# Expert blocks taken two at a time, by seven half-size products in each layer

## The chip, the core and the metric

The kernel runs on one core of one Trainium2 chip. The metric is the device time of one execution, in microseconds; 3 runs of the kernel before gave a median of 2139.81 us, from 2139.24 to 2141.18. All matrices are float32.

## What is computed

A gated cross-attention layer is followed by a gated mixture of experts. Batch is 32, with 112 query rows and 375 context rows each, 256 features wide; there are 16 heads of 64.

```python
x = x + tanh(g_xattn) * attention(context, layernorm(x))   # 16 heads, 487 keys per batch
xf = layernorm(x).reshape(3584, 256)
scores, idx = top_k(softmax(xf @ gate_w), 2)               # 2 of 8 experts per token
h = gelu(xf @ w1[e] + b1[e])                               # 256 -> 1024
y = h @ w2[e] + b2[e]                                      # 1024 -> 256
x = x + tanh(g_ffn) * (scores / sum(scores)) . y[idx]
```

The router sends 7168 rows (3584 tokens, two experts each) to the experts. Evaluated on these inputs, the reference's counts for experts 0 to 7 are 953, 854, 759, 878, 866, 1158, 921 and 779.

## The kernel before

The kernel has two stages, and TensorE's work is written out by hand in one order for the whole kernel. Each other engine, and the SyncE queue (SP) that issues nearly all DMAs, also executes in the order of the program text.

The attention stage is a loop over n = 0 to 127 (32 batches times 4 head groups). Each n has scores, softmax, transposes of the attention, and one part of the key and value projections, in five slots h = 0 to 4 (`slots`, `pe` and `dve` hold what each slot issues). The projections already work on two batches at once by seven products (`seven`, L346): seven products of half-size blocks and a number of sums give what eight products would. Their sums are made on GpSimd (`add`, L394: `kT` and `vv`) and VectorE (L404, L408, L418). Every 128 finished tokens form a slab; `project`, `residual` and `normed` make its attention output, `logits_of` (L577) its eight router logits, and `route_parts` finds its two experts, its gates and its rows' places. An indirect DMA on GpSimd's queue (L673) scatters the rows to `xg` in DRAM, one region for each expert.

The expert stage works on blocks of 128 rows of one expert. 60 blocks always run, and 3 more stand behind a condition at the end (on these inputs the eight counts, rounded up to blocks, come to 60). For a block t, `fetch_rows` (L875) loads its rows from `xg`; `turn_rows` (L893) turns them by two TensorE transposes; `hidden` (L906) makes 8 chunks of 128 hidden features, each a sum of two matmuls with 128 moving columns, and ScalarE applies Gelu while it empties PSUM (L913); `second` (L919) makes 8 matmuls with 256 moving columns into one PSUM tile; VectorE adds the bias (L929) and multiplies by the gate (L935); an indirect DMA on GpSimd's queue adds the rows to the output (L936). In float32 the profile records each matmul twice, and each transpose once. `run` orders TensorE's work as `hidden(t)`, `turn_rows(t + 1)`, `second(t - 1)`.

Expert weights lie in three buffer sets (`weights_of`), used in turn by t % 3. `fetch_weights` (L888) loads w1, b1, w2 and b2 of a block's expert, 1024 KB each for w1 and w2, two blocks ahead. Blocks stand in order of expert, and a DMA is skipped by a condition when its set already holds the expert.

The first six blocks' experts and rows are fixed while attention still runs (`locate_early`). The rest wait for the last two slabs (26 and 27): after the last attention step TensorE runs `project`, the hidden and second layers of blocks 0 to 3 and the router of these slabs, then `locate_late`; the rows of blocks 6 to 9 are fetched, and the regular loop begins.

```python
for t in range(begin, end):
    hidden(t)
    if t + 1 < end:
        turn_rows(t + 1)
    if t > begin or follow:
        second(t - 1)
        combine(t - 1)
```

Of the kernel before, what the change touches and what calls it, by code (L numbers as in the profile page):

```python
# [9 lines left out]
I32 = mybir.dt.int32  # L10
# [13 lines left out]
def kernel(  # L24
# [36 lines left out]
    NSLOT = 2 * T // P + E - 1  # L61
    NE = 6
    NB = 3
    SURE = NSLOT - 3
    AHEAD = 4
# [33 lines left out]
    gwd = dram.tile([E, D], F32, name="gwd")  # L99

# [9 lines left out]
    for e in range(E):  # L110
# [31 lines left out]
    )  # L142

    sums = {
        tag: [const.tile([P, E + 4], F32, name=f"sums{tag}_{n}") for n in range(4)] for tag in "ab"
    }
    for tag in "ab":
        for n in range(4):
            nc.gpsimd.memset(sums[tag][n], 0.0)
# [16 lines left out]
    if True:  # L166
# [20 lines left out]
        lnrows = wqp.tile([4 * KD, P], F32, name="lnrows")  # L187
        b1rows = wqp.tile([E * NF, P], F32, name="b1rows")
        slot = wqp.tile([P, P], F32, name="slot")
# [404 lines left out]
        def route_parts(g, eng):  # L594
# [101 lines left out]
            def stranger_hits(j, e):  # L696
                v["hit"] = rt.tile([P, 2, P], F32, tag="hit", name=f"hit_{j}_{e}", bufs=1)
                nc.vector.tensor_tensor(
                    v["hit"],
                    slot.unsqueeze(1).to_broadcast([P, 2, P]),  # L700
                    v["far"][:, j, e : e + 2].unsqueeze(2).to_broadcast([P, 2, P]),
                    ALU.is_equal,
                )
# [51 lines left out]
        def whole_blocks(tag, rows_, less, up):  # L755
# [6 lines left out]
            nc.vector.tensor_single_scalar(whole, whole, -P, op=ALU.bitwise_and)  # L762
            size = sums[tag][0]
            nc.vector.tensor_copy(size[:, 4:], whole)
# [5 lines left out]
            return size[:, 4:], sums[tag][3][:, 3:]  # L770

        def located(tag, first, start, last):
# [6 lines left out]
            nc.vector.tensor_scalar(begun, first[:, :E], row, None, ALU.is_le)  # L779
# [5 lines left out]
            nc.vector.tensor_tensor(step, start, first[:, :E], ALU.subtract)  # L785
            nc.vector.tensor_tensor(step, step, begun, ALU.mult)
            nc.vector.tensor_reduce(one, step, AX.X, ALU.add)
            nc.vector.tensor_tensor(where[:, 1:2], one, row, ALU.add)
            yield
            nc.vector.tensor_scalar(one, row, float(-NB * P), None, ALU.add)  # L790
            nc.vector.tensor_scalar(begun, first[:, :E], one, None, ALU.is_le)
            nc.vector.tensor_reduce(one, begun, AX.X, ALU.add)
            if last is not None:
                nc.vector.tensor_tensor(one, one, last, ALU.add)
# [3 lines left out]
            if last is not None:  # L798

                nc.vector.tensor_tensor(one, row, first[:, E : E + 1], ALU.is_lt)  # L800
# [6 lines left out]
            found["ab".index(tag)] = wherei  # L807
# [3 lines left out]
        def locate_early():  # L811


            full, first = whole_blocks("a", found.pop("ps"), None, 0.0)
            taken = mp.tile([P, E], F32, name="taken")
            nc.vector.tensor_scalar(
                taken, first[:, :E], -1.0, float(NE * P), ALU.mult, ALU.add
# [3 lines left out]
            found["taken"] = taken  # L821
# [3 lines left out]
            yield from located("a", first, eoff, None)  # L825
            yield

            last = found["last"] = mp.tile([P, 1], F32, name="last")
            begun = mp.tile([P, E], F32, name="begunl")
            nc.vector.tensor_scalar(last, row, float((NE - NB) * P), None, ALU.add)  # L830
            nc.vector.tensor_scalar(begun, first[:, :E], last, None, ALU.is_le)
            nc.vector.tensor_reduce(last, begun, AX.X, ALU.add)
            nc.vector.tensor_scalar(begun[:, :1], row, float(NB * P), None, ALU.is_lt)
            nc.vector.tensor_tensor(last, last, begun[:, :1], ALU.mult)
            yield

        def locate_late():
            _, first = whole_blocks("b", found.pop("ps"), found["taken"], float(P - 1))
            for _ in located("b", first, found["start"], found["last"]):
                pass  # L840


        weights_of = []

        def weight_buffers(pool, n):
            weights_of.append(
                (
                    pool.tile([P, KD, FF], F32, name=f"w1_{n}"),
                    pool.tile([P, NF], F32, name=f"b1_{n}"),
                    pool.tile([P, NF, D], F32, name=f"w2_{n}"),  # L850
                    pool.tile([P, D], F32, name=f"b2_{n}"),
                )
            )

        xs, xsT, hid, psy, ys = {}, {}, {}, {}, {}

        def number(t, n, most, engines=(ET.SP,)):
            late, i = (0, t) if t < NE else (1, t - NE)
            return nc.values_load(  # L859
                found[late][i : i + 1, n : n + 1],  # L860
# [5 lines left out]

        def fetch_rows(t):
            r = number(t, 1, PADS)

            i, new = (t - NE) % (AHEAD + 1 + NE), AHEAD + 1  # L870
            if t < NE or i >= new:
                xs[t] = found["early"].tile([P, C], F32, tag="xs", name=f"xs_{t}", bufs=NE)
            else:
                xs[t] = found["rows"].tile([P, C], F32, tag="xs", name=f"xs_{t}", bufs=new)
            nc.sync.dma_start(xs[t], xg[bass.ds(r, P), :])  # L875

        def fetch_weights(t):

            e = number(t, 0, E - 1)
            new = {"cond": number(t, 2, 1)} if t >= NB else {}  # L880
            w1t, b1t, w2t, b2t = weights_of[t % NB]
            for dst, src in (
                (w1t, w1[bass.ds(e, 1)].rearrange("o (k p) f -> p (o k) f", p=P)),
                (b1t, b1d[bass.ds(e, 1)].rearrange("o p c -> p (o c)")),
                (w2t, w2[bass.ds(e, 1)].rearrange("o (c p) d -> p (o c) d", p=P)),
                (b2t, b2[bass.ds(e, 1), :].to_broadcast([P, D])),
            ):
                nc.sync.dma_start(dst, src, **new)  # L888

        def turn_rows(t, copy=None):  # L890
            ps = ps_m.tile([P, KD, P], F32, tag="m", name=f"ps_x_{t}")
            for k in range(KD):
                nc.tensor.transpose(ps[:, k, :], xs[t][:, k * P : (k + 1) * P], ident)  # L893
            xsT[t] = found["tiles" if t > 0 else "early"].tile(
                [P, KD, P], F32, tag="xsT", name=f"xsT_{t}"
            )
            (copy or nc.vector.tensor_copy)(xsT[t], ps)

        def hidden(t, lo=0, hi=NF):
            w1t, b1t, _, _ = weights_of[t % NB]  # L900
            if lo == 0:
                hid[t] = found["tiles"].tile([P, NF, P], F32, tag="h", name=f"h_{t}")
            for f in range(lo, hi):
                ps = ps_m.tile([P, P], F32, tag="m", name=f"ps_h_{t}_{f}")
                for k in range(KD):
                    nc.tensor.matmul(  # L906
                        ps,
                        lhsT=w1t[:, k, f * P : (f + 1) * P],
                        rhs=xsT[t][:, k, :],
# [3 lines left out]
                nc.scalar.activation(hid[t][:, f, :], ps, AF.Gelu, bias=b1t[:, f : f + 1])  # L913

        def second(t):
            w2t = weights_of[t % NB][2]
# [14 lines left out]
        def combine(t):  # L931
            if t not in ys:
                biased(t)
# [399 lines left out]
```

## Time and profile before

| what | value |
|---|---|
| median of 3 runs | 2139.81 us |
| the profiled execution | 2140.79 us |
| its span | 2139.1 us |
| mean granted TensorE clock | 0.997 |
| busy PE, weight loads (PEld) | 2111.2 us, 1660.0 us |
| busy VectorE (DVE), ScalarE (ACT), GpSimd (POOL) | 1249.4, 1206.4, 708.5 us |
| moved by DMA | 142.63 MB, mean 67 GB/s |

Busy time is the time in which an engine executes. A row of a group gives the line, the engine, the operation, output and inputs, how often it ran, its busy time, the mean length of one in ns, and the idle time ahead of it with what ended that idle time. Starts that follow each other more closely than the mean length show that instructions overlap, so that the pace of a stream is read from the timeline.

### The profile page before, as it was taken

The page shows a single profiled execution, that of the slowest core. Times are in us where ns is not written, and L with a number is a line of the kernel's source. Part 1 is how long each engine was busy: PE and PEld are TensorE (multiplying, and loading weights), DVE is VectorE, ACT ScalarE, POOL GpSimd, SP SyncE. Part 2 cuts the span into 40 slices and gives each one's busy share as a digit, 9 for nine tenths or more (in the row PEclk, how much of TensorE's full clock was granted, in tenths as well). Part 3 has the DMA queues.
Part 4 walks back from the last instruction along what each step waited for, and adds up shares of the span by engine and source line. Part 5 has one row for each costly group of instructions (what it writes and reads, how often), then busy time and mean ns, then how long its engine had stood idle before and what let it go on. Part 6 is the DMA issues. An engine that isn't in the chain of part 4 may idle for free. (4 is left out here: it accounts for less than half of the span.)

```text
span 2139.1 us, 41500 instructions
## 1 busy us (share of the span) xinstructions
PE 2111.2 (99%) x15944; PEld 1660.0 (78%) x15944; DVE 1249.4 (58%) x2784; ACT 1206.4 (56%) x2887; POOL 708.5 (33%) x992
## 2 busy tenths in 40 slices
PE   9999999999999999999999999999999999999998
PEld 5777777777777777777777777777777889999997
DVE  6667676767676767676767676766768521111111
ACT  5666566656665666656656666665655433434433
POOL 4532323343333423442425332533323222222222
PEclk9999999999999999999999999999999999999999
DMA  6693000010000000000000000000002377655552
GB/s 149 183 321 105 18 13 18 13 28 20 16 13 25 25 18 13 30 18 16 13 18 23 28 13 27 14 23 6 6 6 83 102 210 211 166 161 162 155 138 59
DMA packets 116896, 142.63 MB, mean 67 GB/s; under 512 B 15088, under 2 KB 104120, under 8 KB 116568
## 3 DMA queue, kind: packets, MB, share of 16 engines
q1 hardware_dynamic: 104232, 123.57, 18.6%
q0 software_dynamic: 11328, 15.33, 3.9%
q8 instruction: 127, 2.08, 0.4%
q10 hardware_dynamic: 1136, 1.05, 0.2%
q14 instruction: 73, 0.60, 0.1%
HBM read 166.84 MB, written 48.99 MB: 101 GB/s over the span
## 5 line engine op out<-in xcount | busy, mean ns | idle before, releaser
L483 ACT ACTIVATE ex<-ex,rc 112x487 f32<-112x487 f32 x512 | 331.1, 694 | 328.2 <-DVE rc L481 323.3
L459 DVE TENSOR_REDUCE nmx<-ps_s 112x2 f32<-112x974 f32 x256 | 288.0, 1167 | 312.7 <-PE ps_s L449 311.7
L469 ACT ACTIVATE ex<-ps_s,nmx 112x487 f32<-112x487 f32 x512 | 337.2, 666 | 159.7 <-DVE nmx L459 159.0
L490 PEld LDWEIGHTS ps_t<-ident,ex 112*122 112x122 f32 x2048 | 231.8, 138 | 118.3 <-issue 96.9
L913 ACT ACTIVATE h<-ps_h,b 128x128 f32<-128x128 f32 x480 | 175.5, 367 | 260.5 <-PE ps_h L906 220.0
L490 PE MATMUL ps_t<-ident,ex 112*122 112x112 f32 x2048 | 280.8, 259 | 0.2 <-DVE exT L494 0.2
L494 DVE COPY exT<-ps_t 122x448 f32<-122x448 f32 x384 | 237.4, 618 | 37.8 <-PE ps_t L490 36.6
L449 PE MATMUL ps_s<-kT,qT 64*112 64x487 f32 x1024 | 242.0, 591 | 0.0
L394 POOL TENSOR_TENSOR vv<-tmpv,vv 122x512 f32<-122x512 f32 x64 | 81.2, 1269 | 471.9 <-ACT vv L412 377.2
L504 PEld LDWEIGHTS ps_o<-exT,vv 122*64 122x64 f32 (+1 forms) x4096 | 197.6, 136 | 44.7 <-DVE kT L408 32.2
L906 PEld LDWEIGHTS ps_h<-xsT,w 128*128 128x128 f32 x1920 | 224.2, 192 | 6.7 <-ACT h L913 1.8
L906 PE MATMUL ps_h<-xsT,w 128*128 128x128 f32 x1920 | 226.3, 275 | 2.7 <-ACT h L913 1.2
L919 PE MATMUL ps_y<-w,h 128*128 128x256 f32 x960 | 218.6, 381 | 0.0
L504 PE MATMUL ps_o<-exT,vv 122*64 122x112 f32 (+1 forms) x4096 | 211.4, 260 | 0.0
L384 PE MATMUL ps_v<-wkv_s,tT 128*122 128x128 f32 x1536 | 202.0, 274 | 1.2 <-DVE vv L408 1.2
L936 POOL DMA_INDIRECT out_dram<-y,xs x60 | 93.6, 1559 | 314.7 <-DVE y L935 179.4
L919 PEld LDWEIGHTS ps_y<-w,h 128*128 128x128 f32 x960 | 179.3, 192 | 22.4
L378 PE MATMUL ps_k<-tT,wkv_s 128*128 128x487 f32 x378 | 189.4, 583 | 3.4 <-ACT qT L317 3.3
L384 PEld LDWEIGHTS ps_v<-wkv_s,tT 128*122 128x122 f32 x1536 | 181.9, 185 | 4.0 <-issue 1.8
L384 PEld LDWEIGHTS ps_v<-wkv,kvT 128*122 128x122 f32 x1024 | 125.9, 185 | 74.3 <-issue 56.7
L394 POOL TENSOR_TENSOR kT<-tmpk,kT 128x487 f32<-128x487 f32 x63 | 76.9, 1220 | 316.5 <-ACT kT L412 316.4
L418 DVE TENSOR_TENSOR kT<-ps_k,kT 128x487 f32<-128x487 f32 x189 | 124.7, 660 | 47.7 <-PE ps_k L378 42.6
(215 smaller groups left out, 3125.3 us busy)
## 6 DMA issues: line engine op xcount, KB each, us to landing
w<-in_L_ffn_w_dram SPq DMA_DIRECT2D x120, 1024.0 KB
xg<-pad SPq DMA_DIRECT2D x8, 3640.0 KB
cin<-in_ctx_dram SPq DMA_DIRECT2D x32, 336.0 KB
xs<-xg SPq DMA_DIRECT2D x60, 130.0 KB
b<-in_L_ffn_b_dram SPq DMA_DIRECT2D x60, 128.0 KB
xin<-in_x_dram SPq DMA_DIRECT2D x32, 112.0 KB
x<-in_x_dram SPq DMA_DIRECT2D x28, 128.0 KB
out_dram<-x SPq DMA_DIRECT2D x28, 128.0 KB
```

Of the source, the lines that this page charges most:

```text
L378: nc.tensor.matmul(ps, lhsT=w[:, 0, i * P : (i + 1) * P], rhs=x[:, :NK], start=True, stop=True)
L384: nc.tensor.matmul(ps[:, c, :], lhsT=x[:, c * KC : (c + 1) * KC], rhs=w[:, 1, i * P : (i + 1) * P], start=True, stop=True,)
L449: nc.tensor.matmul(ps[:, j, :NK], lhsT=qT[b // 2, i][r, b % 2, :], rhs=kT[b, i][r, :], start=True, stop=True,)
L459: nc.vector.tensor_reduce(nmx[b, i], pss[b, i][:, :, :NK], AX.X, ALU.max, negate=True)
L469: nc.scalar.activation(t[:, j, :NK], ps[:, j, :NK], AF.Exp, bias=nmx[b, i][:, j : j + 1], accum_out=sm[b, i][:, j : j + 1],)
L483: nc.scalar.mul(ex[b, i][:, j, :NK], ex[b, i][:, j, :NK], rc[:, j : j + 1])
L490: nc.tensor.transpose(ps[:, c, :], ex[b, i][:, j, c * KC : (c + 1) * KC], ident[:S, :S])
L494: (nc.scalar.copy if h == 2 else nc.vector.tensor_copy)(exT[b, i, j], ps)
L504: nc.tensor.matmul(ps[y * DH : (y + 1) * DH, r, x * S : (x + 1) * S], lhsT=vv[j][:m, c, x, r, y * DH : (y + 1) * DH], rhs=exT[2 * g + x, i ...
L906: nc.tensor.matmul(ps, lhsT=w1t[:, k, f * P : (f + 1) * P], rhs=xsT[t][:, k, :], start=(k == 0), stop=(k == KD - 1),)
L913: nc.scalar.activation(hid[t][:, f, :], ps, AF.Gelu, bias=b1t[:, f : f + 1])
L919: nc.tensor.matmul(psy[t], lhsT=hid[t][:, f, :], rhs=w2t[:, f, :], start=(f == 0), stop=(f == NF - 1),)
```

## The change

Rows of one expert are taken in 21 pairs of 128-row blocks and 18 single blocks (plus 3 behind the condition). The first 13 pairs (table "a") are placed from the router's counts of 20 slabs, the next 8 (table "b") and the singles (table "c") from the full counts. Each table lists its units in order of expert. Pair 0 is done by plain matmuls with 256 moving columns (`hidden_plain`, `second_plain`). Pairs 1 to 20 use seven products in each layer: `hidden_pair` makes seven products of four matmuls each, 128 moving columns, sums them out of PSUM on VectorE into `h`, and applies Gelu from SBUF, two blocks in one instruction; `rows_sums` makes four combinations of the turned rows on VectorE; `hidden_sums` makes four combinations of the hidden rows on GpSimd; `second_pair` makes seven products accumulated over four chunks and combines them on ScalarE and VectorE.

The products need four sums of each expert's weights in each layer. They are made once in the attention stage, from n = 44 on, in 64 pieces: `piece_in` loads a piece, `piece_sums` makes four GpSimd sums in slots 2 and 3, and `piece_out` stores them to DRAM (`ws1`, `ws2`) at the next n. A pair's weights are thirteen tiles in one buffer each (3.67 MB), loaded by `fetch_first` and `fetch_second` when the expert differs from that of the unit before. `order_` gives the order of the loads. Single blocks use four of the tiles for w1 (256 KB each) and two for w2 (512 KB each), 2.1 MB.

The residual, logits and routing of slabs 26 and 27 and the late tables are cut into a list (`todo`), and one entry is issued at each `between()`: two in each `hidden_pair`, three in each `second_pair`, beginning with four ahead of pair 1. The rest of the attention stage is unchanged.

```diff
+    EARLY = -(-(2 * 20 * P - E * (2 * P - 1)) // (2 * P))
+    LATE = -(-(2 * T - 2 * P * EARLY - E * (2 * P - 1)) // (2 * P))
+    PAIRS = EARLY + LATE
+    NS = (2 * T - 2 * P * PAIRS + E * (P - 1)) // P
+    SURE = NS - 3
+    AHEAD = 3
...
+    ws1 = dram.tile([E, 4, P, FF // 2], F32, name="ws1")
+    ws2 = dram.tile([E, 4, P, NF // 2, P], F32, name="ws2")
...
+            m, i = unit_of(t)
+            r = number(m, i, 1, PADS - 2 * P if t < PAIRS else PADS)
+            pool, n = (found["early"], 1) if t == 0 else (found["rows"], AHEAD + 3)
+            xs[t] = pool.tile([P, 2, C], F32, tag="xs", name=f"xs_{t}", bufs=n)
+            if t < PAIRS:
+                rows_ = xg[bass.ds(r, 2 * P), :].rearrange("(b p) c -> p b c", p=P)
+                nc.sync.dma_start(xs[t], rows_)
...
+        def expert_of(t):
...
+            new = {} if t in (0, 1, EARLY, PAIRS) else {"cond": number(m, i, 2, 1)}
+            return e, new
...
+        def fetch_first(t):
...
+            e, new = found["e", t] = expert_of(t)
+            fetch_biases(t, e, found["weights"], 2)
+            if t < PAIRS:
...
+                order_ = (a11, s2_, s3_, s1_, a22, a12, s4_)
+            else:
+                if t == PAIRS:
+                    new_weights("21", [P, 512], "s3")
+                order_ = [
+                    (n, half_of_w1(e, k, h))
+                    for n, k, h in (("11", 0, 0), ("12", 1, 0), ("21", 0, 1), ("22", 1, 1))
+                ]
+            for n, src in order_:
+                nc.sync.dma_start(wt[n], src, **new)
...
+        def fetch_second(t):
...
+                order_ = (b11, b2x, t4_, t1_, t3_, t2_)
+            else:
+                if t == PAIRS:
+                    new_weights("b1x", [P, NF // 2, D], "t12")
+                order_ = (("b1x", half_of_w2(e, 0, 0, D)), ("b2x", half_of_w2(e, 1, 0, D)))
+            for n, src in order_:
+                nc.sync.dma_start(wt[n], src, **new)
...
+        def rows_sums(t):
+            x = xsT[t]
+            v = xt[t] = found["tiles"].tile([P, 4, P], F32, tag="xt", name=f"xt_{t}")
+            for o, l, r in (
+                (v[:, 0], x[:, 0, 1], x[:, 0, 0]),
+                (v[:, 1], x[:, 1, 1], v[:, 0]),
+                (v[:, 2], x[:, 1, 1], x[:, 0, 1]),
+                (v[:, 3], x[:, 1, 0], v[:, 1]),
             ):
...
+                nc.vector.tensor_tensor(o, l, r, ALU.subtract)
...
+        def hidden_plain(lo, hi):
...
+        def second_plain(b):
...
+        def hidden_pair(t, between):
...
+            x, v = xsT[t], xt[t]
+            H = NF // 2
+            h11, h12, h21, h22 = (h[:, i : i + H, b, :] for i in (0, H) for b in range(2))
...
+            def product(n, w, r):
+                ps = ps_m.tile([P, H, P], F32, tag="m", name=f"ps_h_{t}_{n}")
+                for c in range(H):
+                    nc.tensor.matmul(
+                        ps[:, c, :], lhsT=wt[w][:, c * P : (c + 1) * P], rhs=r, start=True, stop=True
+                    )
+                return ps
+            def gelu(lo):
+                for f in range(lo, lo + H):
+                    nc.scalar.activation(h[:, f], h[:, f], AF.Gelu, bias=bias[t][0][:, f : f + 1])
+            add = nc.vector.tensor_tensor
+            nc.scalar.copy(h11, product(1, "11", x[:, 0, 0]))
+            add(h12, product(6, "s2", v[:, 1]), h11, ALU.add)
+            between()
+            add(h21, product(7, "s3", v[:, 2]), h12, ALU.add)
+            ps = product(5, "s1", v[:, 0])
+            add(h22, ps, h21, ALU.add)
+            add(h12, ps, h12, ALU.add)
+            between()
+            add(h21, product(4, "22", v[:, 3]), h21, ALU.add)
+            gelu(H)
+            add(h11, product(2, "12", x[:, 1, 0]), h11, ALU.add)
+            add(h12, product(3, "s4", x[:, 1, 1]), h12, ALU.add)
+            gelu(0)
...
+        def hidden_sums(t):
...
+            sub = ALU.subtract
+            for o, l, r, op in (
+                (v[0], a21, a22, ALU.add),
+                (a21, a11, a21, sub),
+                (v[1], v[0], a11, sub),
+            ):
+                nc.gpsimd.tensor_tensor(o, l, r, op)
+            last = lambda: nc.gpsimd.tensor_tensor(v[2], a12, v[1], sub)
+            if t > 1:
+                found["last_sum"] = last
...
+        def second_pair(t, between):
...
+            def products(name, parts):
+                ps = ps_s.tile([P, 2, 512], F32, tag="s", name=f"ps_{name}_{t}")[:, 0, :]
+                ps = ps.rearrange("p (n d) -> p n d", d=P)
+                for n, (w, r) in enumerate(parts):
+                    for c in range(H):
+                        nc.tensor.matmul(
+                            ps[:, n, :],
+                            lhsT=w[:, c, :],
+                            rhs=r[:, c, :],
+                            start=(c == 0),
+                            stop=(c == H - 1),
+                        )
+                    if n % 2 == 1:
+                        between()
+                return ps
...
+                nc.scalar.mul(by[:, b], bias[t][1], xs[t][:, b, D : D + 1])
+            ps = products("ya", ((a11, wt["b11"]), (a12, b21), (a22, wt["t4"]), (v[0], wt["t1"])))
+            nc.scalar.copy(q, ps)
+            nc.vector.tensor_tensor(y[:, 0, :P], q[:, 0], q[:, 1], ALU.add)
+            ps = products("yb", ((a21, wt["t3"]), (v[1], wt["t2"]), (v[2], b22)))
+            add = nc.vector.tensor_tensor
+            add(u[:, 0], ps[:, 1], q[:, 0], ALU.add)
+            add(u[:, 1], ps[:, 0], u[:, 0], ALU.add)
+            add(y[:, 1, :P], u[:, 1], q[:, 2], ALU.add)
+            add(y[:, :, P:], u, q[:, 3].unsqueeze(1).to_broadcast([P, 2, P]), ALU.add)
+            add(y[:, 0, P:], ps[:, 2], y[:, 0, P:], ALU.add)
+            for b in range(2):
+                nc.vector.scalar_tensor_tensor(
+                    y[:, b], y[:, b], xs[t][:, b, D : D + 1], by[:, b], ALU.mult, ALU.add
+                )
...
+        def out_pair(t):
...
+            one = add_rows(t, 0, y[:, 0])
+            last_sum = found.pop("last_sum", None)
+            if last_sum:
+                last_sum()
+            other = add_rows(t, 1, y[:, 1])
+            if last_sum:
+                tc.declare_no_dep(other.ins, one.ins, reason="rows of other tokens")
+                found["loose"] = one.ins
...
+            fetch_first(1)
+            fetch_second(1)
+            for t in range(1, 1 + AHEAD):
+                fetch_rows(t)
...
+        pieces = [(l, e, c) for e in range(E) for l in range(2) for c in range(NF // 2)]
+        def piece_in(n):
+            l, e, c = pieces[n]
+            v = found["piece"] = rt.tile([P, 2, 2, P], F32, tag="piece", name=f"piece_{n}", bufs=1)
+            for h in range(2):
+                if l == 0:
+                    lo = h * 512 + c * P
+                    src = w1[e, :, lo : lo + P].rearrange("(k p) f -> p k f", p=P)
+                    nc.sync.dma_start(v[:, :, h, :], src)
+                else:
+                    lo = h * 512 + c * P
+                    src = w2[e, lo : lo + P, :].rearrange("p (j d) -> p j d", j=2)
+                    nc.sync.dma_start(v[:, h, :, :], src)
...
+        def piece_sums(n):
...
+                ops = (
+                    (a22, a21, a22, add),
+                    (a21, a11, a21, sub),
+                    (a11, a22, a11, sub),
+                    (a12, a12, a11, sub),
+                )
...
+        def piece_out(n):
...
+                for k, h, i in ((0, 0, 1), (0, 1, 2), (1, 0, 3), (1, 1, 0)):
+                    nc.sync.dma_start(ws1[e, i, :, c * P : (c + 1) * P], v[:, k, h, :])
+            else:
+                for h, j, i in ((0, 0, 0), (0, 1, 2), (1, 0, 3), (1, 1, 1)):
+                    nc.sync.dma_start(ws2[e, i, :, c, :], v[:, h, j, :])
...
+            k = n - 44
+            if 0 <= k <= len(pieces):
+                if k > 0:
+                    piece_out(k - 1)
+                if k < len(pieces):
+                    piece_in(k)
+                    for h, part in enumerate(piece_sums(k)):
+                        dve[2 + h].append(part)
...
+                weights_ahead()
...
+                fetch_rows(0)
...
+                for h in range(1, 5):
+                    pe[h].append(lambda h=h: hidden_plain(h - 1, h))
...
                 for h in range(4):
...
+                    pe[h].append(lambda h=h: hidden_plain(h + 4, h + 5))
+                pe[4].append(lambda: turn_rows(1))
...
+        r, _ = route_parts(g, nc.vector)
+        todo = [[now]] + [[lambda j=j: residual(j), now] for j in (i, i + 1)]
+        todo += [[part] for parts in extra for part in parts]
+        todo += [[lambda j=j: normed(j), now] for j in (i, i + 1)]
+        todo += [[lambda j=j, e=e: logits_of(j, e, e + 2)] for j in (i, i + 1) for e in range(0, E, 2)]
+        todo += [[part] for part in r[:10]]
+        todo.append([lambda: found.update(ps=counted())])
+        todo += [[part] for part in r[10:]]
+        late = locate_late()
+        todo += [[lambda: next(late)]] * 10
+        def between():
+            if todo:
+                do(todo.pop(0))
...
+        rows_sums(1)
+        second_plain(1)
+        for _ in range(4):
+            between()
         combine(0)
-        combine(1)
-        for t in range(NE, NE + AHEAD):
-            fetch_rows(t)
...
+        for t in range(1, PAIRS):
+            hidden_pair(t, between)
+            fetch_first(t + 1)
+            if t + AHEAD < PAIRS + SURE:
+                if t + AHEAD == EARLY:
+                    while todo:
+                        between()
+                    do(outgoing)
+                    del outgoing[:]
+                fetch_rows(t + AHEAD)
+            turn_rows(t + 1, nc.scalar.copy)
+            if t + 1 < PAIRS:
+                rows_sums(t + 1)
+            hidden_sums(t)
+            if t > 1:
+                second_pair(t - 1, between)
+                out_pair(t - 1)
+                fetch_second(t)
+            if outgoing:
+                outgoing.pop(0)()
...
+        def run(begin, end):
             for t in range(begin, end):
                 hidden(t)
                 if t + 1 < end:
+                    fetch_first(t + 1)
                     turn_rows(t + 1)
...
+                if t == PAIRS:
+                    second_pair(t - 1, lambda: None)
+                    out_pair(t - 1)
+                else:
                     second(t - 1)
                     combine(t - 1)
...
+                fetch_second(t)
+                if t + AHEAD < end:
                     fetch_rows(t + AHEAD)
...
+        run(PAIRS, PAIRS + SURE)
```

## The prediction

> **What bounds the kernel now.** I read the page first: busy time, then the slices of the span.
>
> ```profile
> PE 2111.2 (99%) x15944; PEld 1660.0 (78%) x15944; DVE 1249.4 (58%) x2784; ACT 1206.4 (56%) x2887; POOL 708.5 (33%) x992
> ...
> PEclk9999999999999999999999999999999999999999
> ```
>
> TensorE works 99% of the span at full clock, in both stages; no other engine passes 58%. So only TensorE's work and its waits count. The waits of PE, summed, come to some 20 us, and one of them is 5.2 us, which the timeline places. The next two views are the timeline of PE: a regular block (second to hidden to turn), then the place ahead of the regular loop.
>
> ```profile
> 1900.11 3.62 PE L919 MATMUL ps_y<-w,h 128*128 128x256 f32 x16
> 1903.56 3.73 PE L906 MATMUL ps_h<-xsT,w 128*128 128x128 f32 x32
> 1907.13 0.38 PE L893 MATMUL ps_x<-ident,xs 128*128 128x128 f32 x2
> 1907.35 3.62 PE L919 MATMUL ps_y<-w,h 128*128 128x256 f32 x16
> ```
> ```profile
> 1722.29 3.73 PE L906 MATMUL ps_h<-xsT,w 128*128 128x128 f32 x32
> 1731.27 0.66 PE L893 MATMUL ps_x<-ident,xs 128*128 128x128 f32 x2 [5.25 <-DMA xs<-xg]
> 1731.72 5.37 PE L919 MATMUL ps_y<-w,h 128*128 128x256 f32 x16
> ```
>
> From starts: a block takes 7.24 us. 32 records of 128 moving columns take 1907.13 - 1903.56 = 3.57, 0.1116 each; 16 of 256 take 3.45, 0.216 each: the price goes by columns, with 3% more at 128. Two transposes take 0.22. In the second view PE waits 5.25 us for rows, and the next `second` takes 5.37 instead of 3.62.
>
> The costs of the helpers, from the page's groups:
>
> ```profile
> L394 POOL TENSOR_TENSOR vv<-tmpv,vv 122x512 f32<-122x512 f32 x64 | 81.2, 1269 | 471.9 <-ACT vv L412 377.2
> L936 POOL DMA_INDIRECT out_dram<-y,xs x60 | 93.6, 1559 | 314.7 <-DVE y L935 179.4
> ```
>
> A sum of 512 columns costs GpSimd 1.27 us. The same on VectorE out of PSUM costs 0.68 (group L418, `vv`), one of 256 columns 0.425 (L929).
>
> **What the Trainium skill says.** (1) "SBUF — State Buffer", section "Who interferes with whom": a VectorE instruction with both inputs in SBUF and a GpSimd instruction that reads SBUF exclude each other for their whole length. The trace agrees:
>
> ```profile
> 1660.95 1.27 POOL L394 TENSOR_TENSOR vv<-tmpv,vv 122x512 f32<-122x512 f32 x1 [5.21 <-DVE m L606]
> 1661.39 0.86 DVE L610 TENSOR_TENSOR s<-lg,m 128x16 f32<-128x16 f32 x1
> ```
>
> A comparison that elsewhere takes 0.17 us takes 0.86 and ends with GpSimd's sum, at 1662.2. (2) "TensorE: Matmul & The Clock Gate", "What's actually happening": an idle window of about 3.4 us halves TensorE's clock. The 5.37 above, after 5.25 idle, agrees. (3) "DMA: Bandwidth & Descriptors", "Anatomy of one DMA — SWDGE (gpsimd) path", gives a fixed cost of about 2.0 us, for another issuing path. Here rows issued by SP at 1728.5 were used at 1731.27: 2.8 us. The measured number is used.
>
> **TensorE's work.** A pair by plain blocks costs 4 x 3.5 + 0.44 = 14.48 us. By seven products: each layer has 7 x 4 matmuls, 56 records of 128 columns, 56 x 0.1116 = 6.25 us; two layers and four transposes (0.44) make 12.94. That saves 1.54 us, on 20 pairs 30.8. Pair 0 by 256 columns has 16 matmuls at 2 x 0.216 = 6.91 against 7.14 in the hidden layer: 0.2. The number of blocks stays 60, since pairs take multiples of 256 rows. Together -31 us.
>
> **The old wait.** From the last attention step (1685.4) to PE's end (2131.5) pass 446.1 us. Its work is 3.2 (attend), 6.9 (project), 58 x 3.57, 60 x 3.45, 57 x 0.22 and 0.9 for the router: 437.6. The 8.5 us between are the wait for rows, its slow restart (1.75) and small gaps. The change makes the late tables beside pairs, three units ahead of use, so they go: -8.5.
>
> What comes in their place, along the path:
>
> - **Rows of pair 1.** `others` is issued where memory comes free, 1670.6 in the old trace. Thirteen weight tiles (3.67 MB) go ahead of the rows on SP's queue. In the old trace four saturated 5 us windows, 1750 to 1770, moved 313 to 358 GB/s; at 330 the weights take 11.1 us, the rows 0.8, and with 2.8 us of delay the rows come at about 1686.5. `turn_rows(1)` stands at 1685. Cost +1.5 (0 to 3).
> - **Pair 2.** Frame 1 has no second layer, so `hidden_pair(2)` follows directly, and must wait for pair 1's Gelu, then the ScalarE copy of its own turned rows (one queue). Gelu of 256 columns I take as 0.42 (0.37 for 128, 0.69 for a pass over 487). PE ends the products at 6.25, VectorE the last sum at 7.1, ScalarE eight Gelus and a copy of 0.58 at about 9.8; PE stood at 6.7. Cost +3 (2 to 5); longer idling would also slow the clock.
> - **VectorE in pairs.** Per 12.94 us: seven sums out of PSUM (7 x 0.69 = 4.8), four row differences of 128 columns (estimated 0.27 from 0.425 and 0.68, 1.1 together), the combination of y 2.8: 8.7. GpSimd's four sums (5.1) and two indirect DMAs (3.1) fit. The exclusion adds to VectorE: GpSimd's three first sums start when Gelu ends, where the row differences stand; three waits of 0.9 make 2.7. At 11.4 of 12.94 it fits, with four PSUM buffers as slack. In frames 2 to 8 the router's list comes on top: 16 logits at 0.57, two norms at 0.41, and some 75 small operations at 0.17 make 23 us, 3.3 per frame: 14.7, over by 1.8, seven times: 12. PE's order also holds `places` and `counted`, which wait for VectorE; I count that within. Cost +12 (3, if the waits and the list fall into PE's slack, to 20).
> - **Weights of table b.** By the counts, units 12 to 19 all change expert. A frame moves 3.67 MB of weights, 0.4 of rows and biases, 0.26 of output: 4.33 MB per 12.94 us, 335 GB/s, just what the saturated windows gave. SP issues a taken DMA every 0.73 us (1833.70 to 1834.44 in SP's timeline), a skipped one every 0.43, and 16 with four register loads fill 13 us. `b2x` is freed only by the last product of its pair, and four loads and the next `fetch_first` queue behind it; they land 3 to 4 us ahead of need. So backlog eats slack first. Cost +3 (0 to 15, the latter at 290 GB/s).
> - **Singles.** They cost 7.24 as before. A new expert's first w1 tiles come behind the previous `b2x`, rows, registers and two biases in SP's queue: issue at about 5 us of the frame, landing 3.1 later, needed at 7.25. That is +1.0, for five of seven changes in full, and the two that follow a late one directly get shorter: +5.5 (3 to 11).
> - **Attention stage.** GpSimd gets four sums of 128 columns per n; 0.2 at 8 to 32 elements and 1.22 at 488 give 0.47 each, 1.9 us, 64 times. GpSimd is 33% busy and PE never waits for it there: 0, hidden by that idle time. If the cover fails, see the last rival. `load`, `load_slab` and the residual's stores now stand behind `piece_out` on SP, but were early by whole iterations: 0.
>
> Sum against the profiled execution: 2140.8 - 31 - 8.5 + 1.5 + 3 + 12 + 3 + 5.5 = 2126.3. The median stands 1.0 below that execution, so I predict 2125.
>
> **The rivals.**
>
> - *VectorE keeps up.* For it: its 4.2 us of free time per frame holds the 3.3 of routing, if the exclusion costs little. The term of 12 becomes 2: 2115. Against it: the row differences stand exactly where GpSimd starts. Chance 0.23.
> - *Weights become the bound.* For it: 335 GB/s needed, 5 us windows at 260 seen as well. Frames of 4.33 MB at 290 take 14.9, eight times 2, and later singles: 2125 + 15 = 2140. Against it: slack and faster windows. Chance 0.12.
> - *The piece loop holds GpSimd, ends slower.* Each n, SP stores four tiles, waits until they land, loads the next, waits again. Six issues at 0.44 are 2.6, two landings at 2.0 to 2.8 some 5, sums 1.9: 9.5 to 10, inside an iteration of 12.9. With landings of 4.3 (the median of rows in the trace) and a scatter of 0.96 between the halves it is 14.1; 1.2 us over, 64 times: 2125 + 77 = 2202. GpSimd's `kT` and `vv` sums then come late and PE waits. It decides from 15 / 64 = 0.23 us per iteration. Against it: rows landed 2.8 after issue when nothing else ran. Chance 0.10.
>
> **How the numbers follow.** Forecast (2125, own range 2116 to 2134): 0.55. 0.2% is about what a measurement of this kernel can tell from no change, here 2135.5 to 2144. Forecast and first rival are faster (0.78), the second lies half in each (0.06 faster, 0.06 within), the last is slower (0.10). Range 2107 to 2141: down to the first rival with cheaper singles and weights, up to the second.
>
> **What would show it.** Right: 56 records in 6.25 us per layer and pair; later pairs of table a at 12.9 us per frame; early frames at 14 to 16 with PE waiting on VectorE for PSUM; waits of about 1 us on w1 at single blocks; an unchanged attention stage. Wrong: frames over 13.5 in table b, PE's products above 0.115 per record, or iterations after n = 44 longer than before.

## The result

The changed kernel takes 2266.11 us (median of 4 runs, 2260.71 to 2273.37), against 2140.35 for the kernel before it on the same chips (4 runs, 2139.24 to 2141.18): a ratio of 1.059, with a 95% interval of 1.0558 to 1.0622. It is slower by some 126 us, where 15 us less had been forecast. The profiled execution took 2268.31 us, its span is 2266.6.

### The profile page after: what moved, and what is told of

It is laid out like the page before. It is cut to its first block, busy times and chain, and to the rows that moved or that the text cites. A ratio compares the mean times of both kernels' runs of the same rounds, so it can differ in the third digit from the quotient of the medians.

```text
span 2266.6 us, 44337 instructions
## 1 busy us (share of the span) xinstructions
PE 2139.6 (94%) x16232; PEld 1687.1 (74%) x16232; DVE 1410.6 (62%) x3064; ACT 1202.2 (53%) x2818; POOL 930.1 (41%) x1332
## 5 line engine op out<-in xcount | busy, mean ns | idle before, releaser
L427 DVE TENSOR_TENSOR vv<-ps_v,vv 122x512 f32<-122x512 f32 x192 | 131.5, 685 | 35.5 <-PE ps_v L393 29.9
L1173 ACT ACTIVATE h<-ps_h,b 128x128 f32<-128x128 f32 x144 | 52.9, 368 | 168.1 <-PE ps_h L1166 155.5
L458 PEld LDWEIGHTS ps_s<-kT,qT 64*112 64x112 f32 x1024 | 81.1, 172 | 79.5 <-issue 63.2
L393 PE MATMUL ps_v<-wkv,kvT 128*122 128x128 f32 x1024 | 139.0, 279 | 1.0 <-DVE kT L427 1.0
L1166 PE MATMUL ps_h<-xsT,w 128*128 128x128 f32 x576 | 87.9, 321 | 52.3 <-DMA w<-in_L_ffn_w_dram 52.2
```

The source lines that it names most:

```text
L393: nc.tensor.matmul(ps[:, c, :], lhsT=x[:, c * KC : (c + 1) * KC], rhs=w[:, 1, i * P : (i + 1) * P], start=True, stop=True,)
L427: nc.vector.tensor_tensor(v[at], product(n, w, x), v[at], ALU.add)
L458: nc.tensor.matmul(ps[:, j, :NK], lhsT=qT[b // 2, i][r, b % 2, :], rhs=kT[b, i][r, :], start=True, stop=True,)
```

## The profile after

The same page rows as before, of the changed kernel: busy times, then the slices of the granted TensorE clock.

```profile
PE 2139.6 (94%) x16232; PEld 1687.1 (74%) x16232; DVE 1410.6 (62%) x3064; ACT 1202.2 (53%) x2818; POOL 930.1 (41%) x1332
...
PEclk9999999999999999999999999999998999998889
```

PE has fallen from 99% to 94% of the span, and the clock digits fall below 9 only in the last quarter. So TensorE waits, and then runs slowly for a while, in the expert stage. In the attention stage nothing moved: from 600 to 800 us PE is busy 199.17 of 200 us (199.28 before), although GpSimd rises there from 74.2 to 101.7 us.

Since the last attention step starts at 1685.39 (1685.43 before), the loss can be placed exactly. I cut the stage at three points of PE's timeline: the first product of pair 1, the first matmul of the first single block (unit 21), and the end. A half-pair is one layer of a pair, that is seven products; a turn is the transposes of one unit's rows; a frame runs from the first hidden product of one unit to that of the next. The work of each stretch, from the prediction's prices, is: up to pair 1, 17.0 us; then 39 half-pairs of 6.25, 20 turns and the router's 0.9, together 253.2; then the second layer of pair 20, 18 single blocks (7.02 each) and 17 turns, 136.3.

| stretch | work | changed kernel | lost |
|---|---|---|---|
| to pair 1 | 17.0 | 17.15 | 0.1 |
| pairs, 1702.54 to 2031.83 | 253.2 | 329.3 | 76.1 |
| singles, 2031.83 to 2259.0 | 136.3 | 227.2 | 90.9 |

The sum of work, 406.5, is 39.6 below the 446.1 of before: the 31 of TensorE's work and the 8.5 of the old wait. The loss of 167.1 less 39.6 is 127.5, the difference of the two spans. The wait for rows that the view of before showed is gone too. The gain was there in full; four times as much was lost beside it. PE's waits make 104 us of the 167 (42 in the stretch of pairs, 62 in that of singles). In the rest its records took longer than their price: the mean granted clock was 0.93 in the pairs and 0.87 in the singles.

What PE waits for, summed (us, times, longest), in the first three rows:

```profile
PE ps_h L1166 <- DMA w<-in_L_ffn_w_dram: 52.2, 19, 5.5
PE ps_h L1055 <- DMA w<-in_L_ffn_w_dram: 13.3, 7, 2.9
PE ps_y L1181 <- DMA w_b1x<-in_L_ffn_w_dram: 9.9, 4, 2.9
```

PE waits for weights, above all those of single blocks (L1166). That looks like slow transfers, and isn't. Here are a few late single blocks on PE's timeline, all of expert 7, so that no weight moves at all:

```profile
2230.18 3.96 PE L1166 MATMUL ps_h<-xsT,w 128*128 128x128 f32 x32 [1.36 <-DMA w<-in_L_ffn_w_dram]
2233.98 0.38 PE L967 MATMUL ps_x<-ident,xs 128*128 128x128 f32 x2
2234.20 1.89 PE L1181 MATMUL ps_y<-w_b1x,h 128*128 128x256 f32 x8
2235.93 1.89 PE L1181 MATMUL ps_y<-w_b2x,h 128*128 128x256 f32 x8
2239.17 3.96 PE L1166 MATMUL ps_h<-xsT,w 128*128 128x128 f32 x32 [1.36 <-DMA w<-in_L_ffn_w_dram]
```

A block takes 8.99 us, not 7.24, and PE waits 1.36 us each time for loads that are skipped. The reason stands in the queue of SP and in VectorE's timeline of the same block:

```profile
2234.37 0.34 SPq L895 DMA_DIRECT2D b<-b1d  x1
2238.31 0.33 SPq L896 DMA_DIRECT2D b<-in_L_ffn_b_dram  x1
2238.97 1.36 SPq L933 DMA_DIRECT2D w<-in_L_ffn_w_dram  x4
```
```profile
2237.85 0.42 DVE L1039 TENSOR_TENSOR y<-ps_y,b 128x256 f32<-128x256 f32 x1 [3.03 <-PE ps_y L1181]
```

SP issues the b1 load of the next unit at 2234.37 and then stands for 3.6 us before the b2 load (L896). It goes on at 2238.31, just when VectorE's bias sum of the previous block ends (2237.85 + 0.42). `fetch_biases` has two buffers for b2: the next unit's b2 overwrites that of the previous unit, and its last reader, `combine`, comes at the end of the frame. In SP's queue the four w1 loads stand behind it, and even a skipped one must be passed before PE may use its tile: PE starts 0.20 us after the first of them. So the frame has become a ring: second layer ends 2237.82, bias sum 2238.27, b2 load 2238.31, w1 loads from 2238.97, PE 2239.17. Where the expert changes the loads are real and take their landing time on top:

```profile
2051.84 0.33 SPq L896 DMA_DIRECT2D b<-in_L_ffn_b_dram  x1
2052.51 2.42 SPq L933 DMA_DIRECT2D w<-in_L_ffn_w_dram  x4
```
```profile
2056.69 5.63 PE L1166 MATMUL ps_h<-xsT,w 128*128 128x128 f32 x24 [5.34 <-DMA w<-in_L_ffn_w_dram]
```

PE waits 5.34 us and then restarts slowly: 24 records take 5.63 us instead of 2.84. The pairs have the same wait, with another reader. The waits of SP's queue at L896, summed:

```profile
SPq L896 <- ACT by L1130: 117.9, 19, 14.3
SPq L896 <- DVE y L1039: 108.0, 16, 9.8
```

In pairs the last reader of b2 is ScalarE's `by` (L1130), which stands behind the next pair's Gelus.

**Theory.** SP's wait for the b2 buffer, with all weight loads queued behind it, is the main loss. **Rival.** The single-buffered weights come too late by themselves, by bandwidth or landing time. A second question is what VectorE costs in the pairs: PE also shows waits on its sums (L1066, L1068: 9.3 us).

## Experiments

All times are medians, with the kernel before on the same chip at 2140.4 to 2141.1. Pairs and singles are the stretches of the table above, cut in the same way in the profiled execution. That one lay within 2.6 us of the median, but in e6 (2236.5) 7.5 us below it.

| kernel | us | ratio to before (95%) | pairs, lost | singles, lost |
|---|---|---|---|---|
| changed kernel | 2266.11 | 1.0558 to 1.0622 | 329.3, 76.1 | 227.2, 90.9 |
| e1_b2_later | 2164.25 | 1.0091 to 1.0124 | 308.7, 55.5 | 146.7, 10.4 |
| e2_no_refetch | 2192.75 (one run) | | 314.7, 61.5 | 166.7, 30.4 |
| e3_sums_from_psum | 2148.73 | 1.0021 to 1.0044 | 292.0, 38.8 | 147.4, 11.1 |
| e4_list_moved | 2126.82 | 0.9922 to 0.9956 | 268.8, 15.6 | 144.9, 8.6 |
| e5_rows2_early | 2123.73 | 0.9906 to 0.9939 | 267.7, 14.5 | 144.5, 8.2 |
| e6_without_b2_edit | 2243.99 | 1.0466 to 1.0501 | 304.9, 51.7 | 220.4, 84.1 |
| e7_gate_early | 2238.81 | 1.0437 to 1.0472 | 306.8, 53.6 | 220.7, 84.4 |

**e1: only the b2 load goes later.** No buffer is added.

```diff
 def fetch_biases(t, e, pool, n):
...
-    nc.sync.dma_start(b2t, b2[bass.ds(e, 1), :].to_broadcast([P, D]))
     bias[t] = b1t, b2t
+    if t == 0:
+        fetch_b2(t, e)
+
+def fetch_b2(t, e):
+    nc.sync.dma_start(bias[t][1], b2[bass.ds(e, 1), :].to_broadcast([P, D]))
...
 def fetch_second(t):
...
     for n, src in order_:
         nc.sync.dma_start(wt[n], src, **new)
+    fetch_b2(t, e)
```

> The only edit: the load of the bias row b2 of a unit leaves the start of fetch_first and goes to the end of fetch_second of the same unit, about one frame later, when the last reader of the buffer that it overwrites is long done. Theory (SP waits at the b2 load, 226 us in the changed kernel, and every weight load queued behind it is issued at the end of its frame): the SP waits at the b2 load disappear, frames of single blocks go from 8.9-11 us back to 7.25-8.3, the stretch of singles from 230 us to about 147, the pairs from 326 to 271-286; time 2135 (2120 to 2160). Rival (the weights themselves are late: bandwidth of the transfers, single-buffered tiles): the waits of PE on w stay in sum over 60 us and the time stays above 2230.

It measured 2164.25, 102 us less, for one load moved. SP's waits at the b2 load are gone (none on `by` is left), and PE's waits on w1 in the singles fall from 52.2 us to 2.5:

```profile
SPq L901 <- DVE y L1044: 1.5, 9, 0.2
```
```profile
PE ps_h L1171 <- DMA w<-in_L_ffn_w_dram: 2.5, 5, 0.9
```

The same weights are moved from the same buffers, so the rival falls. The singles came out as expected (146.7), the pairs did not: 308.7 instead of 271 to 286, which put the time 4 us above the expected range. So the pairs hold a second loss of some 50 us that the theory doesn't cover.

**e2: no weights fetched again.** The flag "new expert" is always 0, so that later units use wrong weights.

```diff
-nc.vector.tensor_tensor(where[:, 2:3], one, where[:, 0:1], ALU.not_equal)
+nc.vector.tensor_tensor(where[:, 2:3], one, one, ALU.not_equal)
```

> The changed kernel with the flag 'new expert' always 0: after the first unit of each table no weights are fetched again (each of these DMAs is still queued on SP, and skipped), so later units are computed with the wrong expert's weights; the bias loads and their place stay. It leaves out nearly all weight traffic of the units. Theory (wait at the b2 load): the SP waits at the b2 load stay over 150 us in sum, single blocks still take about 9 us a frame, and the time only falls by the extra of the frames that change expert, some 11 x 5 us: 2205 (2180 to 2235). Rival (bandwidth or latency of weight transfers): nothing has to land any more, so the time falls to 2115-2135.

It measured 2192.75, inside the theory's range and 58 us above the rival's. With next to no weight traffic, SP still waits at the b2 load for most of the time that it did, and from the third single block on the frames still take 8.99 to 9.03 us:

```profile
SPq L896 <- ACT by L1130: 141.7, 19, 15.2
SPq L896 <- DVE y L1039: 59.0, 16, 4.7
```

The landing of real loads, begun that late, accounts for the other 73 us (60.5 of it in the singles). It is one run, but the distances are large.

**e7: the reader goes earlier instead of the load later.**

```diff
+def gated(t):
+    by = found["tiles"].tile([P, 2, D], F32, tag="by", name=f"by_{t}", bufs=1)
+    for b in range(2):
+        nc.scalar.mul(by[:, b], bias[t][1], xs[t][:, b, D : D + 1])
+    found["by"] = by
...
     nc.scalar.copy(h11, product(1, "11", x[:, 0, 0]))
+    if t > 1:
+        gated(t - 1)
...
```

> The changed kernel with one edit: the two ScalarE products of b2 and the row weights of pair t-1, the last readers of b2 of t-1, go from the start of second_pair to just after the first copy of hidden_pair of t, some 8 us earlier in the frame; all loads stay where they are. Theory (SP waits for exactly this reader in the pairs, and for the sum in combine in the singles): the SP waits at the b2 load on the ScalarE product fall from 118 us to under 25, those on the sum in combine stay at about 108; the stretch of pairs falls from 329 us to about 309, that of the singles stays at 227; time 2246 (2238 to 2254). Rival (the wait at b2 is a label for something else that SP waits for in pairs): time 2258 or more, the pairs stay above 322.

It measured 2238.81, at the low end of the theory's range, with 306.8 in the pairs as expected and the singles 6 us lower than expected. SP's waits are as the theory names them:

```profile
SPq L896 <- DVE y L1039: 103.6, 16, 9.6
SPq L896 <- ACT by L1047: 19.8, 8, 3.5
```

The reader was moved and no load was, and the pairs gained 22.5 us, what e1 gave them (20.6). So the wait is on this reader, in the pairs; the singles, whose reader stayed, keep most of their loss (84.4 of 90.9).

**e3: VectorE's row differences read PSUM.** In e1 the pairs run at a steady 14.0 us a frame where 12.94 was forecast. VectorE and GpSimd in one of them:

```profile
1868.41 0.29 DVE L988 TENSOR_TENSOR xt<-xsT 128x128 f32<-128x128 f32 x1 [2.65 <-ACT xsT L976]
1868.74 1.40 DVE L988 TENSOR_TENSOR xt<-xsT,xt 128x128 f32<-128x128 f32 x1
1870.06 0.28 DVE L988 TENSOR_TENSOR xt<-xsT 128x128 f32<-128x128 f32 x1
1870.26 1.35 DVE L988 TENSOR_TENSOR xt<-xsT,xt 128x128 f32<-128x128 f32 x1
```
```profile
1868.72 1.27 POOL L1099 TENSOR_TENSOR hs<-h 128x512 f32<-128x512 f32 x1 [1.75 <-ACT xsT L976]
1870.06 1.40 POOL L1099 TENSOR_TENSOR h<-h 128x512 f32<-128x512 f32 x1
```

A difference of 0.29 us takes 1.40 when GpSimd's sum has begun just ahead of it, and ends 0.15 us after that sum. This is the exclusion that the Trainium skill states ("SBUF — State Buffer", "Who interferes with whom") for a VectorE instruction with two SBUF inputs and a GpSimd instruction that reads SBUF.

```diff
-    x = xsT[t]
+    x, ps = xsT[t], found["turned"]
...
-        (v[:, 0], x[:, 0, 1], x[:, 0, 0]),
-        (v[:, 1], x[:, 1, 1], v[:, 0]),
-        (v[:, 2], x[:, 1, 1], x[:, 0, 1]),
-        (v[:, 3], x[:, 1, 0], v[:, 1]),
+        (v[:, 0], ps[:, 0, 1], x[:, 0, 0]),
+        (v[:, 1], ps[:, 1, 1], v[:, 0]),
+        (v[:, 2], ps[:, 1, 1], x[:, 0, 1]),
+        (v[:, 3], ps[:, 1, 0], v[:, 1]),
```

> e1_b2_later and one more edit: the four row differences of a pair take their left operand from PSUM, so that VectorE no longer has two inputs in SBUF there and does not exclude GpSimd's sums. Theory (the exclusion of VectorE and GpSimd is a real part of what is lost in the pairs, the sums of v come late for products 5 to 7): each difference falls from up to 1.3 us to about 0.3, and the time falls below e1_b2_later by 3 to 12 us. Rival (VectorE's work in a pair has slack enough, PE does not wait for it once weights are in time): same as e1_b2_later within 2 us.

It measured 2148.73, which is 15.5 below e1 and 3 beyond the expected gain; the stretch of pairs gives 16.7. The groups of these differences, from 1700 to 1970 us (count | busy, mean ns | idle before), in e1 and in e3:

```profile
L988 DVE TENSOR_TENSOR xt<-xsT,xt 128x128 f32<-128x128 f32 x34 | 31.2, 918 | 0.6
```
```profile
L989 DVE TENSOR_TENSOR xt<-ps_x,xt 128x128 f32<-128x128 f32 x36 | 10.3, 286 | 0.6
```

With one input in PSUM the mean falls from 918 to 286 ns, and the frames from pair 9 on take 12.94 us, as forecast (one takes 13.1).

**e4: the router's list moves inside the frame.** What e3 still loses in the pairs lies before 1840 us, in the frames that carry the list. One instruction of it, and GpSimd at that moment (e3):

```profile
1805.83 2.27 DVE L788 TENSOR_SCALAR begunb<-sumsb,row 128x8 f32<-128x8 f32 x1
1808.14 0.16 DVE L789 TENSOR_REDUCE whereb<-begunb 128x1 f32<-128x8 f32 x1
```
```profile
1805.20 1.56 POOL L1022 DMA_INDIRECT out_dram<-y,xs  x1 [4.07 <-DVE y L1148]
1806.22 1.84 POOL L1101 TENSOR_TENSOR hs<-h,hs 128x512 f32<-128x512 f32 x1
```

An operation on 8 columns lasts 2.27 us, until GpSimd's fourth sum is done; behind it in VectorE's order stands the sum L1074 that frees PSUM for PE. The operation starts ahead of that sum, while GpSimd's indirect DMA (L1022) still runs, so the DMA may have held it too; no run separates the two. The edit gives `hidden_pair` an empty `between` and issues the two parts after the turn:

```diff
-    hidden_pair(t, between)
+    hidden_pair(t, lambda: None)
...
     turn_rows(t + 1, nc.scalar.copy)
+    between()
+    between()
```

> e3_sums_from_psum, and the two parts of the router's list that each early frame issued between the PSUM sums of hidden_pair are issued after them instead, between the copy of the turned rows and the row differences, where VectorE idles 2.6 us a frame; the two parts between the second layer's products stay. Same work. Theory (the place decides: a small operation of the list that meets GpSimd's fourth sum holds VectorE 2.3 us ahead of the sums that free PSUM; VectorE is busy 100 of 137 us in the early frames, so it isn't full): the early frames fall from 15.1 us on the mean to about 13.7, time 2136 (2130 to 2142). Rival (the amount decides: VectorE has too much work in these frames, wherever it stands): waits of PE on h move into the next frame, time 2145 to 2150.

(The parts that stay are three a frame, not two.) It measured 2126.82, 22 us below e3 and below the expected range: the pairs gain 23.2. The expectation took e3's early frames at 15.1 us on the mean; the eight from pair 1 to pair 9 take 17.1, and 14.2 in e4. The work is the same and only its place differs, so the rival falls. The same operation on VectorE is short now, with GpSimd idle (e5, which shares this edit):

```profile
1795.36 0.22 DVE L788 TENSOR_SCALAR begunb<-sumsb,row 128x8 f32<-128x8 f32 x1
```

PE's waits on the sums fall only from 16.5 to 6.6 us. Most of the rest is the clock: over the stretch of pairs it is granted at 0.94 in e3 and at 1.00 in e4. In e3 two waits followed each other with one product between:

```profile
1825.03 1.16 PE L1061 MATMUL ps_h<-xsT,w 128*128 128x128 f32 x8 [1.62 <-DVE h L1072]
1828.67 2.08 PE L1061 MATMUL ps_h<-xsT,w_s 128*128 128x128 f32 x8 [2.48 <-DVE h L1074]
```

The product after the first takes 1.16 us, that after the second 2.08, and the next ones run slow too. In e4 the second wait is gone, and no such slow product appears in the pairs.

**e5: the rows of pair 2 are turned ahead of pair 1.**

```diff
+turn_rows(2)
+rows_sums(2)
 for t in range(1, PAIRS):
...
-    turn_rows(t + 1, nc.scalar.copy)
+    if t > 1:
+        turn_rows(t + 1, nc.scalar.copy)
...
-    if t + 1 < PAIRS:
+    if 1 < t < PAIRS - 1:
         rows_sums(t + 1)
```

> e4_list_moved, and the rows of pair 2 are turned, copied by VectorE and differenced before the products of pair 1, so that they don't wait for pair 1's Gelus on ScalarE. Theory (pair 2's wait of 3.0 us and its slow restart of 3 us are the price of the missing second layer in frame 1): the wait goes and the time falls by 5 (3 to 7) from e4. Rival (pair 2's later products then wait for the sums of pair 1 on VectorE, or the turn waits for PSUM): within 1.5 us of e4.

The wait of pair 2 is gone from the trace. The time, 2123.73, is 3.1 below e4, the low end of what was expected. But the intervals of the two overlap, and in the profiled executions the way from the last attention step to PE's end is only 1.1 us shorter, so the gain is not established. (One turn, 0.44 us, has moved out of the stretch of pairs.) In e4 that wait was 2.66 us (3.01 in e3) and already had no slow restart behind it, so less was left to take. This is the best version: 17 us below the kernel before.

**e6: the two edits of VectorE's work without the move of b2.** It is e4 with the b2 load in its old place.

> e4_list_moved with the b2 load back in its old place: that is the changed kernel with the two edits of VectorE's work alone (differences from PSUM, list parts moved). Theory (the b2 wait and VectorE's delays are two losses in series: the first sits at the end of a frame, the second in its middle): the time falls from the changed kernel by the same 38 to 40 us that the two edits gave after e1, to 2226 (2218 to 2236). Rival (they lie beside each other: what VectorE delays is covered by the weights' lateness): time 2245 to 2266.

It measured 2243.99, 22 us below the changed kernel, not 38 to 40. That is outside the first forecast's range, and 1 us below the rival's: VectorE's delays and the late weights lie partly in series and partly beside each other. What each of them "cost" in the changed kernel therefore depends on the order in which they are removed. The place of b2 is worth 102 us if it is changed first and 117 if last (2243.99 to 2126.82); in the pairs it is 20.6 or some 36 (304.9 to 268.8).

## Why the prediction was wrong

- **Singles, +5.5: the step that failed.** It said that a new expert's w1 loads come behind "the previous `b2x`, rows, registers and two biases in SP's queue" and are issued at about 5 us of the frame. The two biases were priced as two issues. The second of them is a wait on the buffer of the unit before last, whose reader ends after the frame's last matmul: in the frame shown above, which began at 2043.86, the w1 loads were issued 8.65 us into it (2052.51) instead of 5. The term measured 90.9. With b2 out of the way it is 10.4 (e1), 11.1 (e3) and 8.6 (e4), against the 3 to 11 given for it. The prediction asked of the weights when their tiles come free, and never asked it of b2.
- **Weights of table b, +3.** The same wait cost the pairs 20.6 to some 36, and "frames over 13.5 in table b", a sign of being wrong, came true: from pair 13 on they take 14.0 to 17.1 us. The transfers themselves cost nothing there: with b2 moved, no product of a pair's hidden layer waits for a weight tile (e3, e4). The rival "weights become the bound" named the tiles that PE waits for, but not the cause.
- **VectorE in pairs, +12.** Wrong in size: of the 55.5 lost by the pairs in e1 about 6 are pair 2, and by difference some 49 are this term. "At 11.4 of 12.94 it fits, with four PSUM buffers as slack" fails in the late frames: exclusion made them 14.0 us and cost 16.7 in all (e3). VectorE was not full there (busy 127.5 of 165.5 us in e1, from 1845 to 2010.5), so a sum of its work per frame could not show this. The list was costed by its amount, 3.3 us a frame; what it cost beyond that came from its place, where one small operation lasts 2.3 us beside GpSimd's work, ahead of sums that PE needs (23.2, e4). The prediction saw the exclusion and put it at the row differences only. What is left in e4 after pair 2, about 13, is near the 12 forecast, and early frames of 14.6 to 16.4 us from pair 3 on fit its sign "early frames at 14 to 16".
- **Pair 2, +3.** The mechanism and the wait are right (3.01 us, on ScalarE's copy); the slow restart, named but not counted, doubled it: the products after it took 2.9 us longer than usual.
- **Rows of pair 1, +1.5.** No wait: 0.
- **TensorE's work, -31, and the old wait, -8.5.** Both right; a half-pair without waits is seen here in the changed kernel, seven products from 1849.97 to the next pair's first product at 1856.22, 6.25 us:

```profile
1849.97 1.06 PE L1114 MATMUL ps_ya<-w_b,h 128*128 128x128 f32 x8
...
1855.33 1.06 PE L1114 MATMUL ps_yb<-w_b2x,hs 128*128 128x128 f32 x8
1856.22 1.06 PE L1055 MATMUL ps_h<-xsT,w 128*128 128x128 f32 x8
```

- **Attention stage, 0.** Right; the rival that ended slower (the piece loop) did not happen. Slower came from a place that no rival named.

That e4 lands 2 us from the forecast does not make the forecast right: e4 has three edits that the forecast did not know it needed.

## What to carry to other kernels

For every DMA in an ordered queue ask which earlier reader frees its destination and where in the frame that reader stands; then ask it of the smallest tile first, because a 1 KB bias row holds up megabytes queued behind it. A wait that PE shows on a weight tile says only which load came last: read the issuing queue's own timeline before blaming bandwidth. Place small VectorE operations with two SBUF inputs where GpSimd is idle, or give them an input in PSUM, and count with the small ones ahead of a sum that frees a buffer.

## What the runs showed of the hardware

- A skipped DMA is not free in its queue: four skipped w1 loads take 1.36 us of SP's time, and PE's first matmul on them began only when the first had been passed (2238.97 to 2239.17).
- An 8-column operation whose first input is in SBUF and second a per-partition operand (L788, `TENSOR_SCALAR`) took 2.27 us beside GpSimd's indirect DMA and sum, against 0.22 with GpSimd idle.
- The length of a single wait doesn't tell whether the clock falls. In e4 a wait of 2.66 us was followed by 8 records in 1.16 us and 24 in 2.84, at a granted clock of 1.00. In the changed kernel a shorter one, of 2.29 us, was followed by 8 records in 1.16 us but then by 24 in 4.47, at a granted 0.68:

```profile
1711.20 1.16 PE L1061 MATMUL ps_h<-xsT,w 128*128 128x128 f32 x8 [2.66 <-ACT xsT L977]
1712.20 2.84 PE L1061 MATMUL ps_h<-xt,w_s 128*128 128x128 f32 x24
```
```profile
1969.82 1.16 PE L1055 MATMUL ps_h<-xsT,w 128*128 128x128 f32 x8 [2.29 <-DMA w<-in_L_ffn_w_dram]
1970.78 4.47 PE L1055 MATMUL ps_h<-xt,w_s 128*128 128x128 f32 x24
```

The Trainium skill ("TensorE: Matmul & The Clock Gate", "What's actually happening") speaks of an idle window of about 3.4 us; here the clock fell after less. What decides it was not isolated.
